# Two layers of graph attention and weighted sums on one core: GpSimd takes over the range guard's products, the sums' factors and the low features' split

## The chip, the cores and the metric

The kernel runs on one core of a Trainium2 chip. The metric is the device time of one execution in microseconds; the median of three runs is given. A separate profiled execution leaves the trace that is read below. The engines are named as in the profile: PE (matrix multiply), DVE (VectorE), ACT (ScalarE), POOL (GpSimd), SP (which issues the large loads).

## The reference

`x` is 3327 x 64, `adj` a symmetric 0/1 matrix of 3327 x 3327 with about 0.5% ones. Layer 0 aggregates in hyperbolic space with attention, layer 1 sums a node's last hundred neighbours with weights that halve from one neighbour to the next. Both have a layer norm and a ReLU ahead and a residual.

```python
# layer 0, h = relu(layernorm(x))
x_t = logmap0(h, c)                                   # c = 1 / r^2
left, right = x_t @ w_att[:D, 0], x_t @ w_att[D:, 0]
adj_att = sigmoid(left[:, None] + right[None, :] + b_att[0]) * adj
x_local = logmap(h[:, None, :], h[None, :, :], c)
support_t = einsum('ij,ijd->id', adj_att, x_local)
x = x + proj(expmap(h, support_t, c), c)
# layer 1, h = relu(layernorm(x))
support = h @ weight
rank = cumsum(adj != 0, axis=1); deg = rank[:, -1:]
k = minimum(deg, 100.0); pos = rank - (deg - k)
w = mask * where(pos > 0, 0.5 ** (k - pos), 0.0)
x = x + w @ support + bias
```

## The kernel before

The 3328 padded nodes are 26 blocks of 128. The output nodes i are cut into four strips of 8, 8, 6 and 4 blocks; inside a strip the source nodes j run from block 25 down to block 0. A round is one block j of a strip (two in the last strip), and there are 26 + 26 + 26 + 13 = 91 rounds. For a round the work is:

- SP loads the adjacency tile `ad` (`load`, five buffers).
- DVE turns it into a mask (`edges`, L622), PE counts later neighbours with it (`count`, L633 and L634), and DVE or ACT, mostly in turn, keeps the count (`read`, L656, L658, L660).
- ACT makes the attention as a tanh (`sigmoids`, L671); DVE multiplies it by the adjacency (`pair_one`, L676).
- PE forms a pairwise quantity from features of i and j (`products`, L688 and L689); ACT applies two Gelu functions to it (`gelu`, L881); DVE multiplies it in (`pair_two`, L681).
- PE sums it against the table `hw` of j (`total`, L701). `hw` holds, for each node, 64 scaled features and one more factor.

Only the stretch ahead of the rounds and their beginning are touched by the change. There, per-node statistics are made by small DVE operations on 128 x 26 elements (L790 to L802): `x2`, the squared norm, `bal`, `babs`, `nrm`. Then the features `zf` (L805) are made for groups of blocks: `first_i` (0 to 7), `last_j` (24, 25), `high` (16 to 23) and `low` (8 to 15). Each group is stored in half precision twice: `nu`, a copy, and `nz`, a half precision copy (`nz[.., 0]`) with what it leaves over (`nz[.., 1]`, a difference). For `low` these are L911 on DVE, L926 on ACT and L933 on DVE. PE transposes them into PSUM (`turned_to`, L813), and DVE and ACT copy the transposes to `ju` (L817) and `jz` (L818), which `products` reads. For block group `first_i` six DMAs on POOL's queue (L867) move `iz` and `iu` into `jz` and `ju`.

The factors of the table are `wn` (L913, L916) and `opx` (L914); L915 writes the table's last column, and seven products on POOL (L919) its 64 features, in the order in which the rounds need them.

The range guard decides whether the fast path may stand: it takes the largest `nrm`, the largest `c x2 nrm`, and the largest and smallest `bal` over all real nodes (`node` is 1 for them and 0 for the padding). `range_steps` makes these in the tile `st` in four portions of DVE work (L980 to L990), which `advance` hands out to rounds 2 and after; `in_range` brings the four columns to one flag in the last rounds.

The order of PE, DVE and ACT is the order of the program text, written out by hand (`manual_schedule` with `IN_ORDER`). POOL's and SP's instructions are ordered by a scheduler, so a line of POOL's work can stand earlier or later than its place in the text. `post` (L1021) makes the per-node end of each strip with many small POOL instructions beside the next strip's rounds.

Of the kernel before, what the change touches and what calls it, by code (L numbers as in the profile page):

```python
# [12 lines left out]
F32 = mybir.dt.float32  # L13
# [6 lines left out]
ALU = mybir.AluOpType  # L20
AX = mybir.AxisListType
PSUM = bass.MemoryType.PSUM

P = 128
N = 3327
NB = 26
NP = NB * P
D = 64
# [11 lines left out]
BIG, LATER, ACT, POOL = 4, 99, 100, 101  # L40
# [35 lines left out]
WA = 4.016768702491527  # L76
# [372 lines left out]
def fast(ctx, tc, x, adj_t, r, w_att, b_att, weight, bias, out, flag):  # L449

    nc = tc.nc
    V, A, G, T = nc.vector, nc.scalar, nc.gpsimd, nc.tensor
# [47 lines left out]
    node = const.tile([P, NB], F32, name="node")  # L500
# [4 lines left out]
    def scalar_col(name):  # L505
        return const.tile([P, 1], F32, name=name)

    inv_r, c_c, sqc, absr, maxnorm, c2_c, m2c, p2c, negc, zs_c, za_c, f_c = (
        scalar_col(n) for n in ("inv_r", "c_c", "sqc", "absr", "maxnorm", "c2_c", "m2c", "p2c", "negc", "zs_c", "za_c",
                                "f_c"))  # L510
# [15 lines left out]
    def wide(t, n):  # L526
# [3 lines left out]
    x2, bal, balm, nrm, left, right, sv, su, sk, ih = (  # L530
        const.tile([P, NB], F32, name=n)
        for n in ("x2", "bal", "balm", "nrm", "left", "right", "sv", "su", "sk", "ih"))
    hw = const.tile([P, NB, D + 1], F32, name="hw")
# [9 lines left out]
    post_pool = ctx.enter_context(tc.tile_pool(name="post", bufs=1))  # L543
    st = const.tile([P, 4], F32, name="st")
# [119 lines left out]
    def sigmoids(n, of=slice(None)):  # L664

        S = strips[rounds[n][0]]
        if n not in sg_of:
            sg_of[n] = work.tile([P, FMAX], F32, name="sg", bufs=SGB)
        sg = sg_of[n]
        for j in js(n)[of]:  # L670
            A.activation(part(n, sg, j), S.left[:, : S.F], AF.Tanh, bias=right[:, j : j + 1], scale=0.5)  # L671

    def pair_one(n):
        w = span(n)
        sg = sg_of[n][:, :w]
        V.scalar_tensor_tensor(sg, sg, 1.0, ad_of.pop(n)[:, :w], op0=ALU.add, op1=ALU.mult)  # L676

    def pair_two(n):
        w = span(n)
        sg = sg_of[n][:, :w]  # L680
        V.scalar_tensor_tensor(sg, pq_of.pop(n)[:, :w], WD, sg, op0=ALU.add, op1=ALU.mult)  # L681
# [39 lines left out]
    def small(name):  # L721
        return pre.tile([P, NB], F32, name=name)
# [10 lines left out]
    v, y = v2[:, 0], y2[:, 0]  # L733
# [41 lines left out]
    zf = pre.tile([P, NB, D], F32, name="sq")  # L775
    nz = pre.tile([P, NB, 2, D], F16, name="d")
# [97 lines left out]
    high, low = slice(16, 24), slice(8, 16)  # L874
# [35 lines left out]
    features(low)  # L910
    V.tensor_copy(nu[:, low, :D], zf[:, low])  # L911
    wn, opx = small("wn"), small("opx")
    V.tensor_scalar(wn, nrm, WA / 2, None, op0=ALU.mult)  # L913
    V.tensor_scalar(opx, x2, c_c, 1.0, op0=ALU.mult, op1=ALU.add)  # L914
    V.tensor_mul(hw[:, :, D], opx, wn)  # L915
    V.tensor_mul(wn, wn, y)  # L916
    for b in (24, 20, 16, 12, 8, 4, 0):
        n = min(4, NB - b)
        G.tensor_mul(hw[:, b : b + n, :D], rl[:, b : b + n], wide(wn[:, b : b + n], n))  # L919
# [3 lines left out]
    sigmoids(0)  # L923
    kept(p3, high, 0)
    pair_one(0)
    A.copy(nz[:, low, 0], zf[:, low])  # L926
    pair_two(0)
    for j in js(1):
        count(1, j)
    products(1)  # L930
    A.copy(left_b[:, : strips[0].F], pl[:, : strips[0].F])
    strips[0].left = left_b
    V.tensor_sub(nz[:, low, 1], zf[:, low], nz[:, low, 0])  # L933
    sigmoids(1)
    gelus(1)
    logits((high,))
# [39 lines left out]


    def range_steps():
        t1 = post_pool.tile([P, NB], F32, name="st1")
        V.tensor_mul(t1, nrm, node)  # L980
        V.tensor_reduce(st[:, 0:1], t1, AX.X, ALU.max)
        yield 2
        V.scalar_tensor_tensor(t1, x2, c_c, t1, op0=ALU.mult, op1=ALU.mult)
        V.tensor_reduce(st[:, 1:2], t1, AX.X, ALU.max)
        yield 2
        V.tensor_mul(t1, bal, node)
        V.tensor_reduce(st[:, 2:3], t1, AX.X, ALU.max)
        yield 2
        V.tensor_reduce(st[:, 3:4], t1, AX.X, ALU.min)
        V.tensor_scalar(st[:, 3:4], st[:, 3:4], -1.0, None, op0=ALU.mult)  # L990

    def in_range():
        pf = ps.tile([P, P], F32, name="pc")
# [270 lines left out]
    def add(j, wt, n):  # L1264
# [5 lines left out]
                 start=j == order[0], stop=j == NB - 1)  # L1270

    stages, rest_of_ahead = [Stage(range_steps())], last_of_ahead()
    range_end = in_range()
    load(LOADS)
# [175 lines left out]
@with_exitstack  # L1450
def gnn_kernel(
    ctx: ExitStack,
    tc: tile.TileContext,
    x: bass.AP,
    adj_t: bass.AP,
    r: bass.AP,
    w_att: bass.AP,
    b_att: bass.AP,
    weight: bass.AP,
    bias: bass.AP,  # L1460
    out: bass.AP,
):
    keep = ctx.enter_context(tc.tile_pool(name="keep", bufs=1))
    flag = keep.tile([1, 1], I32, name="flag")
    args = (x, adj_t, r, w_att, b_att, weight, bias, out)
    with ExitStack() as inner:
        fast(inner, tc, *args, flag)
    cond = tc.nc.values_load(flag)
    with tc.If(cond > 0):
        with ExitStack() as inner:  # L1470
            general(inner, tc, *args)
# [28 lines left out]
```

## Time and profile before

| what | us |
|---|---|
| three runs, median | 398.67 |
| lowest and highest of them | 398.03 and 398.76 |
| the profiled execution, its own time | 398.52 |
| its span, first to last instruction | 396.7 |
| busy PE, DVE, ACT | 350.1, 364.2, 348.5 |
| busy POOL | 143.2 |

The span is 1.8 us shorter than the time of that execution. The page gives each engine's busy time as a mean over stages that differ: a set-up to about 36 us, the rounds of four strips to about 345 us, and the second layer's sums to the end. DVE with 92% of the span, PE and ACT with 88% each are close to each other; POOL has 36%. A row of the timeline shows the start, the duration, the engine and the line, the operation, output and inputs with their shapes. The durations of neighbours on one engine overlap a little, so the distance between two starts is the better measure of what an instruction takes from its engine.

### The profile page before, as it was taken

The page shows a single profiled execution, that of the slowest core. Times are in us where ns is not written, and L with a number is a line of the kernel's source. Part 1 is how long each engine was busy: PE and PEld are TensorE (multiplying, and loading weights), DVE is VectorE, ACT ScalarE, POOL GpSimd, SP SyncE. Part 2 cuts the span into 40 slices and gives each one's busy share as a digit, 9 for nine tenths or more (in the row PEclk, how much of TensorE's full clock was granted, in tenths as well). Part 3 has the DMA queues.
Part 4 walks back from the last instruction along what each step waited for, and adds up shares of the span by engine and source line. Part 5 has one row for each costly group of instructions (what it writes and reads, how often), then busy time and mean ns, then how long its engine had stood idle before and what let it go on. Part 6 is the DMA issues. An engine that isn't in the chain of part 4 may idle for free.

```text
span 396.7 us, 4776 instructions
## 1 busy us (share of the span) xinstructions
PE 350.1 (88%) x1460; PEld 149.3 (38%) x1460; DVE 364.2 (92%) x551; ACT 348.5 (88%) x401; POOL 143.2 (36%) x279
## 2 busy tenths in 40 slices
PE   0067999999999899999998999999977899999892
PEld 0053333333333333333333354444433333344362
DVE  3999999999999999999999999999998999798941
ACT  2589999999999999999999999999988899697510
POOL 8136200000000166932133674851248678234100
PEclk9999999999999999999999999999999999999996
DMA  7314555455557455545445445555644430000022
GB/s 208 150 43 132 177 141 145 142 161 156 159 159 211 133 154 158 159 127 164 137 129 151 121 134 161 153 136 151 192 133 135 122 107 0 2 0 1 2 47 48
DMA packets 23299, 49.00 MB, mean 124 GB/s; under 512 B 8789, under 2 KB 9245, under 8 KB 23265
## 3 DMA queue, kind: packets, MB, share of 16 engines
q1 hardware_dynamic: 20993, 47.66, 41.2%
q10 hardware_dynamic: 1808, 0.46, 0.6%
q0 software_dynamic: 464, 0.49, 0.5%
q8 instruction: 13, 0.21, 0.2%
q14 instruction: 21, 0.17, 0.1%
HBM read 46.40 MB, written 0.87 MB: 119 GB/s over the span
## 4 chain that ended last, share of the span: by engine, by line
DVE 42%; ACT 25%; issue 15%; PE 13%; POOL 2%; DMA 1%; POOLq 0%; DVEq 0%; ACTq 0%
DVE sg L676 12%; DVE sg L681 12%; ACT pq L881 10%; ACT sg L671 7%; PE po L701 4%; DVE mask L622 3%; ACT behind_lo L656 2%; ACT behind_hi L656 2%; PE pc L633 1%; DMA x_sb<-in_x 1%; DVE behind_hi L660 1%; DVE behind_lo L660 1%; PE pc L634 1%; PE pq L688 1%; PE pq L689 1%
## 5 line engine op out<-in xcount | busy, mean ns | idle before, releaser
L881 ACT ACTIVATE pq<-pq 128x1024 f32<-128x1024 f32 (+1 forms) x182 | 173.7, 960 | 2.6 <-PE pq L689 0.8
L701 PE MATMUL po<-sg,hw 128*65 128x512 f32 (+1 forms) x364 | 159.7, 562 | 0.1
L681 DVE SCALAR_TENSOR_TENSOR sg<-pq,sg 128x1024 f32<-128x1024 f32 (+1 forms) x91 | 103.7, 1140 | 3.1 <-ACT pq L881 2.4
L676 DVE SCALAR_TENSOR_TENSOR sg<-sg,ad 128x1024 f32<-128x1024 f32 (+1 forms) x91 | 105.5, 1160 | 0.1
L671 ACT ACTIVATE sg<-left_b,right 128x1024 f32<-128x1024 f32 (+2 forms) x103 | 101.7, 987 | 0.0
L701 PEld LDWEIGHTS po<-sg,hw 128*65 128x65 f32 x364 | 48.9, 137 | 67.1 <-issue 52.8
L633 PE MATMUL pc<-mask,ca 128*128 128x512 bf16 (+1 forms) x175 | 63.5, 363 | 8.9 <-ACT behind_hi L656 3.5
L688 PE MATMUL pq<-iu,ju 71*128 71x512 f16 (+1 forms) x182 | 66.5, 366 | 1.1 <-ACT jz L818 0.8
L634 PE MATMUL pc<-mask,cb 128*128 128x512 bf16 (+1 forms) x182 | 64.7, 366 | 1.6 <-DVE mask L622 1.6
L689 PE MATMUL pq<-iz,jz 128*128 128x512 f16 (+1 forms) x182 | 65.0, 364 | 0.0
L622 DVE TENSOR_SCALAR mask<-ad 128x1024 bf16<-128x1024 f32 (+1 forms) x91 | 59.2, 652 | 0.0
L634 PEld LDWEIGHTS <-cb 128*128 128x128 bf16 x182 | 17.7, 97 | 47.5 <-issue 34.6
L1108 POOL CAST w<-mask 128x1 f32<-128x1 bf16 x3 | 1.5, 505 | 89.3 <-DVE mask L622 89.2
L633 PEld LDWEIGHTS <-ca 128*128 128x128 bf16 x175 | 17.1, 98 | 30.5 <-issue 18.3
L688 PEld LDWEIGHTS <-ju 71*128 71x128 f16 x182 | 17.8, 98 | 23.1 <-DVE sg L681 5.4
L1269 PEld LDWEIGHTS <-s 128*128 128x128 f16 x182 | 17.7, 98 | 21.3 <-DVE s L1093 2.3
L689 PEld LDWEIGHTS <-jz 128*128 128x128 f16 x182 | 17.9, 98 | 18.7 <-issue 1.1
L660 DVE TENSOR_SCALAR behind_lo<-pc 128x1024 uint8<-128x1024 f32 (+2 forms) x24 | 24.4, 1019 | 0.3 <-PE pc L634 0.3
L656 ACT ACTIVATE behind_hi<-pc 128x1024 uint8<-128x1024 f32 (+2 forms) x25 | 21.8, 873 | 1.6 <-PE pc L634 1.6
L656 ACT ACTIVATE behind_lo<-pc 128x1024 uint8<-128x1024 f32 (+2 forms) x24 | 20.8, 865 | 0.0
L852 PE MATMUL pq<-id,nui 128*71 128x128 f16 x8 | 1.0, 312 | 21.4 <-ACT nzi L826 21.4
L660 DVE TENSOR_SCALAR behind_hi<-pc 128x1024 uint8<-128x1024 f32 (+2 forms) x15 | 14.8, 985 | 0.9 <-PE pc L634 0.7
(344 smaller groups left out, 382.6 us busy)
## 6 DMA issues: line engine op xcount, KB each, us to landing
ad<-in_adj_t SPq DMA_DIRECT2D x65, 512.0 KB, 3.6
ad<-in_adj_t SPq DMA_DIRECT2D x26, 384.0 KB, 3.2
out<-o SPq DMA_DIRECT2D x6, 128.0 KB, 1.9
left_b<-left_d SPq DMA_DIRECT2D x1, 512.0 KB, 4.5
x_sb<-in_x ACTq DMA_DIRECT2D x1, 416.0 KB
x_sb<-in_x SPq DMA_DIRECT2D x1, 416.0 KB, 5.2
left_b<-left_d SPq DMA_DIRECT2D x1, 384.0 KB
jz<-iz POOLq DMA_DIRECT2D x2, 128.0 KB, 2.6
```

The costliest lines, as they stand in the source:

```text
L622: V.tensor_scalar(*args, 0.0, None, op0=ALU.not_equal)
L633: T.matmul(S.pc[:, f0:f1], ca, S.before[:, f0:f1], start=False, stop=True, skip_group_check=True)
L634: T.matmul(S.pc[:, f0:f1], cb, now[:, f0:f1], start=S.first, stop=True, skip_group_check=True)
L656: A.activation(kept, of, AF.Relu, scale=128.0 if j in JD else 1.0)
L660: V.tensor_scalar(kept, S.pc[:, : S.F], 0.0, None, op0=ALU.max)
L671: A.activation(part(n, sg, j), S.left[:, : S.F], AF.Tanh, bias=right[:, j : j + 1], scale=0.5)
L676: V.scalar_tensor_tensor(sg, sg, 1.0, ad_of.pop(n)[:, :w], op0=ALU.add, op1=ALU.mult)
L681: V.scalar_tensor_tensor(sg, pq_of.pop(n)[:, :w], WD, sg, op0=ALU.add, op1=ALU.mult)
L688: T.matmul(part(n, pq, j, f0, f1), ju[:KB, j, :], S.iu[:, f0:f1], start=True, stop=False)
L689: T.matmul(part(n, pq, j, f0, f1), jz[:, j, :], S.iz[:, f0:f1], start=False, stop=True)
L701: T.matmul(po[: D + 1, : f1 - f0], hw[:, j, :], part(n, sg_of[n], j, f0, f1), start=j == NB - 1, stop=j == 0)
L881: A.activation(pq, pq, AF.Gelu, scale=scale)
```

## The change

Three pieces of work move to POOL.

- The four instructions of the sums' factors (L913 to L916) are issued on POOL in place of DVE. The products of the table, already on POOL, come from them.
- The low features' half precision copy moves from ACT (L926) to POOL, and the difference from DVE (L933) to POOL, directly behind it.
- The range guard's products are made on POOL, side by side in one tile `tops` of 128 x 4 x 26. One DVE reduction makes all four columns of `st`; the smallest `bal` becomes the largest of the negated products. The portions of DVE work become one.

```diff
-    V.tensor_scalar(wn, nrm, WA / 2, None, op0=ALU.mult)
-    V.tensor_scalar(opx, x2, c_c, 1.0, op0=ALU.mult, op1=ALU.add)
-    V.tensor_mul(hw[:, :, D], opx, wn)
-    V.tensor_mul(wn, wn, y)
+    G.tensor_scalar(wn, nrm, WA / 2, None, op0=ALU.mult)
+    G.tensor_scalar(opx, x2, c_c, 1.0, op0=ALU.mult, op1=ALU.add)
+    G.tensor_mul(hw[:, :, D], opx, wn)
+    G.tensor_mul(wn, wn, y)
     for b in (24, 20, 16, 12, 8, 4, 0):
         n = min(4, NB - b)
         G.tensor_mul(hw[:, b : b + n, :D], rl[:, b : b + n], wide(wn[:, b : b + n], n))
...
     pair_one(0)
-    A.copy(nz[:, low, 0], zf[:, low])
+    G.tensor_copy(nz[:, low, 0], zf[:, low])
+    G.tensor_sub(nz[:, low, 1], zf[:, low], nz[:, low, 0])
     pair_two(0)
...
     strips[0].left = left_b
-    V.tensor_sub(nz[:, low, 1], zf[:, low], nz[:, low, 0])
     sigmoids(1)
...
     def range_steps():
-        t1 = post_pool.tile([P, NB], F32, name="st1")
-        V.tensor_mul(t1, nrm, node)
-        V.tensor_reduce(st[:, 0:1], t1, AX.X, ALU.max)
-        yield 2
-        V.scalar_tensor_tensor(t1, x2, c_c, t1, op0=ALU.mult, op1=ALU.mult)
-        V.tensor_reduce(st[:, 1:2], t1, AX.X, ALU.max)
-        yield 2
-        V.tensor_mul(t1, bal, node)
-        V.tensor_reduce(st[:, 2:3], t1, AX.X, ALU.max)
-        yield 2
-        V.tensor_reduce(st[:, 3:4], t1, AX.X, ALU.min)
-        V.tensor_scalar(st[:, 3:4], st[:, 3:4], -1.0, None, op0=ALU.mult)
+        tops = post_pool.tile([P, 4, NB], F32, name="tops")
+        G.tensor_mul(tops[:, 0], nrm, node)
+        G.tensor_scalar(tops[:, 1], x2, c_c, None, op0=ALU.mult)
+        G.tensor_mul(tops[:, 1], tops[:, 1], tops[:, 0])
+        G.tensor_mul(tops[:, 2], bal, node)
+        G.tensor_scalar(tops[:, 3], tops[:, 2], -1.0, None, op0=ALU.mult)
+        yield LATER
+        V.tensor_reduce(st, tops, AX.X, ALU.max)
+        yield LATER
```

In the changed build the orders of PE, DVE and ACT are those of before without the moved instructions, and with the one reduction at the place of the guard's second portion. On POOL the scheduler puts the factors, the guard's products and then the seven products of the table directly behind the first small instructions, and ahead of the six DMAs of L867; the low features' copy and difference stand behind these DMAs. On SP one adjacency load stands ahead of the third strip's own loads instead of between them.

## The prediction

> **What bounds the kernel now.** I read the busy time by stretches first, to see which engine is full where the change acts and which is full afterwards.
>
> ```profile
> 18.00:24.00 6.00, 2.50 (x21) 2.30 (x22) 5.62 (x29) 4.39 (x11) 0.51 (x2) 1.00 0.01 1
> 24.00:29.30 5.30, 4.37 (x51) 2.73 (x50) 5.06 (x20) 4.45 (x7) 3.20 (x6) 1.00 0.31 79
> 29.30:36.20 6.90, 4.99 (x43) 2.42 (x42) 6.83 (x12) 6.42 (x7) 6.69 (x7) 1.00 0.27 78
> 43.80:127.00 83.20, 82.27 (x284) 31.04 (x283) 82.39 (x92) 82.40 (x85) 1.80 (x2) 1.00 0.54 160
> 127.00:208.00 81.00, 79.91 (x283) 30.57 (x282) 80.80 (x84) 80.27 (x86) 33.29 (x64) 1.00 0.51 148
> ```
>
> The columns are the stretch, its length, then PE, PEld, DVE, ACT and POOL. In the set-up, 18 to 36 us, DVE is full (5.62 of 6.00, 5.06 of 5.30, 6.83 of 6.90). POOL works 0.51 us before 24 us and is full from 29.3 to 36.2. After 43.8 us three engines are full at once. Which one sets the pace is in ACT's timeline, followed by the only line that the waits of ACT hold between 44 and 210 us:
>
> ```profile
> 46.72 1.14 ACT L671 ACTIVATE sg<-left_b,right 128x1024 f32<-128x1024 f32 x1
> 47.76 2.06 ACT L881 ACTIVATE pq<-pq 128x1024 f32<-128x1024 f32 x2
> 49.73 1.14 ACT L671 ACTIVATE sg<-left_b,right 128x1024 f32<-128x1024 f32 x1
> 50.77 1.01 ACT L656 ACTIVATE behind_hi<-pc 128x1024 uint8<-128x1024 f32 x1
> 51.67 2.06 ACT L881 ACTIVATE pq<-pq 128x1024 f32<-128x1024 f32 x2
> 53.65 1.14 ACT L671 ACTIVATE sg<-left_b,right 128x1024 f32<-128x1024 f32 x1
> ...
> ACT behind_hi L656 <- PE pc L634: 0.3, 1, 0.3
> ```
>
> Two rounds take ACT 53.65 - 46.72 = 6.93 us, exactly its own work, and in 166 us it waits 0.3 us. So from 43.83 us (that one wait) to about 208 us ACT is the bound. What the set-up gains or loses moves ACT's start and is carried on whole; what DVE saves in the rounds only makes DVE wait. The chain of waits draws the range guard's steps (L980 to L990, 51 to 63 us) through DVE, but the even period shows that ACT doesn't feel them.
>
> The set-up's path, from the same chain: DVE's small operations to 19.2, ACT, PE's transposes, DVE's copy of iu at 23.80 (queued behind L622, which ended at 23.68, so with 0.1 us of slack), DVE without a gap to 36.23, and then the copy of the low features' transposes:
>
> ```profile
> 33.09 0.90 DVE d L933
> 34.50 1.13 DVE sg L676
> 36.26 1.02 ACT jz L818
> ```
>
> Everything up to 43.83 hangs on that copy at 36.26.
>
> Last, what DVE and POOL do to each other:
>
> ```profile
> 26.88 0.68 DVE L904 TENSOR_TENSOR d<-sq,d 128x512 f16<-128x512 f32 x1
> 33.01 0.99 DVE L933 TENSOR_TENSOR d<-sq,d 128x512 f16<-128x512 f32 x1
> 353.06 1.22 DVE L1380 TENSOR_SCALAR wt<-behind_lo 128x1664 uint16<-128x1664 uint16 x1
> 364.69 0.87 DVE L1078 TENSOR_TENSOR rt_last<-rn_last 128x4 f32<-128x4 f32 x1 [0.42 <-POOL rn_last L1078]
> ```
>
> L904 and L933 are one operation on one shape: 0.68 us with POOL issuing DMAs, 0.99 us beside the table's products. L1380 takes 0.58 us elsewhere and 1.22 beside a POOL product of 384; a product of four elements, 0.16 us elsewhere, took 0.87 beside POOL's subtraction of 364.64. The loss is no slower rate, but a wait for the POOL instruction to end.
>
> **What the Trainium skill says.** SBUF — State Buffer, section "Who interferes with whom": DVE's second read port is GpSimd's only one; a DVE instruction with two SBUF inputs, or in a two-port mode, and a GpSimd instruction that reads SBUF exclude each other: "the other fully blocks". The four rows agree (+0.31, +0.64, +0.71 us). It also says that a PSUM operand keeps DVE out of this: L681 at 31.87 took its usual 1.23 us beside the products. Perfetto Trace Analysis, "GPSIMD Engine Instruction", advises the spacing of starts rather than durations for GpSimd; I do so. GPSIMD Engine Reference, "Engine selection", has GpSimd about two times slower for two inputs; the products here are far off that path, so the ratio isn't used.
>
> **The change, part by part.** The instruction order of the changed build shows more than the diff: on POOL the eleven small operations (four of the factors, five of the guard, two older copies) and all seven table products now stand ahead of the six DMAs of L867. Before, the products came behind them.
>
> (a) Removed from DVE: L913 to L916, 28.54 to 29.24 = 0.70 us; L933, 0.90 us in place. Removed from ACT: the copy at L926, 0.52 us start to start (31.46 to 31.98). Beside the products at their old place DVE also loses 0.19 us (L676 at 30.44: 1.40 against 1.21) which goes; L933's 0.31 is in its 0.90.
>
> (b) The guard: eight DVE instructions of 0.15 to 0.24 us at four places against one reduction of 128x4x26 (estimate 0.25 us; L981 takes 0.18 for 26 elements). About 1.2 us of DVE, worth 0, since ACT sets the pace there. Bounds: 0, and a gain of 1.2 if DVE did set it.
>
> (c) The small operations on POOL. Inputs arrive at 17.94 (x2), 18.22, 18.45 and 18.80 us (nrm). POOL's small instructions start 0.16 us apart when independent (320.10 to 320.26) and 0.29 apart when one needs the other (146.50, 146.80, 147.09). Five and six of them: 2.5 us, with DVE between them some 3.3, so the products begin at about 21.3 us and not 29.41. DVE's chain of 18.0 to 19.2 meets some six of them; bounded by 0 (POOL's four of 15.7 to 16.3 left no trace on DVE) and 6 x 0.12 = 0.7; I take 0.3.
>
> (d) The products, the term that decides. Their starts in narrow windows are 0.57 us apart when free (30.15, 30.72), and L933, started at 33.01 against a product of 32.84, ran as if begun at 33.31: a product holds the port 0.47 us. Seven of them (the first is half as long) now fall between 21.3 and some 27 us. There DVE has L840, L843, L844, L845, L846 (two SBUF inputs), L841, L842 (half precision copies, uncertain) and L622 (the mask[...]) in a row, and L860 behind them. Whoever waits is served when the other ends, as at 353.06 (DVE, POOL, DVE), so each DVE instruction pays up to one product. Most: 7 x 0.47 = 3.2 us. Least: the products run while DVE reads PSUM or waits for PE (1.4 us from 23.8 on) and it is 0.5, as at the old place. I take six meetings at 0.38, between the 0.30 of L933 and the full 0.47: 2.3 us. With (c), L860 comes 2.6 us later, and everything behind it: PE's products, the gelu of round 0, sigmoids.
>
> (e) What (a) gives back of it on the path. At L676 of round 0 (30.44) DVE would be 2.6 - 0.7 = 1.9 later, but ACT's sigmoid, which lost nothing, 2.6: ACT is late next. ACT then drops L926 (0.52) and its 0.34 us wait for L817: its copy to left_b, the sigmoid and gelu of round 1 and the copy at 36.26, which starts 0.14 us after that gelu, are 2.6 - 0.52 - 0.34 - 0.14 = 1.6 us later. DVE: L676 of round 1 follows the sigmoid, L817 ends about 37.6, within the 37.86 of that copy.
>
> (f) The low features on POOL: products done about 26.5, the six DMA issues took 3.2 us (24.78 to 27.99) and start when iu is there, 27.2, so to 30.5; the low features are ready at 28.17 + 2.6 = 30.8; copy 0.5 (estimate from L489's 0.34 for 128 columns), subtraction 1.0 to 1.8 (364.64: 0.91 for 384; 1.54 and 1.82 for 512 with waits). Done at 32.4 to 33.3, 4 us ahead of the copy of their transposes: cost 0. Its cover gone, each us late would be a us. L926's and L933's readers are PE's transposes alone. The six DMAs, 2.5 us later, fill ju and jz for blocks 0 to 7, which the first strip reads last (about 100 us): 0. On SP one adjacency load moves ahead of the third strip's loads near 120 us; the data are needed some 10 us later: 0.
>
> **Sum.** +0.3 + 2.3 - 1.0 = +1.6 us. Profiled execution: 398.52 us (span 396.7 and 1.8 around it) to 400.1; the median of the runs shown is 398.67, 0.15 above: 400.3. The bounds: (c) 0 to 0.7 and (d) 0.5 to 3.2, less 1.0, give -0.5 to +2.9.
>
> **Rivals.** "Same" is within 0.2%, 0.8 us, about what this kernel's measurement can tell.
> 1. Forecast: the products hold DVE up at 21 to 27 us; +0.9 to +2.9, 399.6 to 401.6. For it: the four rows and the order. Against: no row shows a run of small DVE instructions between products. Chance 0.64.
> 2. The products slip into DVE's waits and PSUM reads. It decides once fewer than three meetings of 0.4 are left: 0.3 + 0.9 - 1.0, about +0.2: 398.9, from -0.7 to +0.7. Chance 0.16.
> 3. The other side, faster: DVE keeps the port from 18 to 29 us and POOL waits, so only (a) counts. The point is a loss in (c) and (d) under 0.2 us; then -0.86 to -1.0, and up to -2.2 if the guard's 1.2 counts also: 397.7, from 396.5. For it: DVE is never idle there. Against: a POOL instruction that has begun isn't interrupted (364.69). Chance 0.14.
> 4. POOL is so late that the transposes wait for its subtraction: 402 to 404, chance 0.06.
>
> Faster 0.14, same 0.17 (case 2 and the edge of 1), slower 0.69. The range leaves out case 3 and most of 4: 398.0 to 401.9; the forecast's own is 399.6 to 401.6.
>
> **What would show it.** The first product on POOL near 21 us; L843 to L846 or L622 with 0.3 to 0.5 us above their times; L860 at 25.5 to 27 against 23.80; the copy of L818 for the low features near 37.9 against 36.26; ACT's period still 6.93 and its start in the rounds shifted alike; DVE with idle time behind 66 us. If L860 stands at 24 and that copy before 36, case 3 holds. If ACT's period shortens, (b) was wrong.

## The result, and the profile after

The changed kernel takes 400.76 us (median of ten runs, 400.35 to 402.29) against 399.12 us (ten runs, 397.44 to 400.80) for the kernel before beside it: 1.0056 times as long, 95% interval 1.0036 to 1.0076, so about 1.4 to 3.0 us slower. (The ratio is taken over all these runs; it is not the quotient of the two medians, which is 1.0041, or 1.64 us.) The profiled execution took 400.45 us with a span of 398.6, against 398.52 and 396.7 before.

The busy time by stretches of the changed kernel, in the columns of the forecast (start and end, length, PE, PEld, DVE, ACT, POOL, granted clock, DMA share, GB/s):

```profile
18.00:24.00 6.00, 2.50 (x20) 2.10 (x21) 5.92 (x23) 4.27 (x11) 5.74 (x16) 1.00 0.00 1
24.00:29.30 5.30, 3.30 (x28) 1.63 (x28) 5.05 (x16) 2.53 (x5) 3.70 (x8) 1.00 0.20 44
43.80:127.00 83.20, 82.07 (x282) 31.50 (x286) 82.36 (x87) 82.09 (x84) 2.34 (x4) 1.00 0.54 163
```

DVE is full at 18 to 24 us as before, but works on 23 instructions there in place of 29. In 24 to 29.3 us PE does 28 matmuls in place of 51, and ACT 2.53 us of work in place of 4.45: both wait. From 43.8 us on the columns are close to those of before.

What fills DVE is in its own timeline. The kernel before, then the changed one:

```profile
21.46 0.69 DVE L840 TENSOR_TENSOR nzi<-sq,nzi 128x512 f16<-128x512 f32 x1 [0.16 <-ACT nzi L826]
22.07 0.23 DVE L841 COPY nu<-nu 128x78 f16<-128x78 f16 x1
22.17 0.23 DVE L842 COPY nu<-nu 128x78 f16<-128x78 f16 x1
22.28 0.28 DVE L843 TENSOR_TENSOR d<-sq,d 128x128 f16<-128x128 f32 x1
22.47 0.18 DVE L844 SCALAR_TENSOR_TENSOR g<-g,s 128x26 f32<-128x26 f32 x1
22.56 0.24 DVE L845 SCALAR_TENSOR_TENSOR g<-g,g 128x26 f32<-128x26 f32 x1
22.92 0.25 DVE L846 SCALAR_TENSOR_TENSOR g<-g,g,g 128x26 f32<-128x26 f32 x1
23.08 0.69 DVE L622 TENSOR_SCALAR mask<-ad 128x1024 bf16<-128x1024 f32 x1
23.80 0.69 DVE L860 COPY iu<-pq 71x1024 f16<-71x1024 f16 x1
```

```profile
21.19 0.78 DVE L840 TENSOR_TENSOR nzi<-sq,nzi 128x512 f16<-128x512 f32 x1
21.90 0.63 DVE L841 COPY nu<-nu 128x78 f16<-128x78 f16 x1
22.41 0.22 DVE L842 COPY nu<-nu 128x78 f16<-128x78 f16 x1
22.52 0.69 DVE L843 TENSOR_TENSOR d<-sq,d 128x128 f16<-128x128 f32 x1
23.14 0.59 DVE L844 SCALAR_TENSOR_TENSOR g<-g,s 128x26 f32<-128x26 f32 x1
23.65 0.65 DVE L845 SCALAR_TENSOR_TENSOR g<-g,g 128x26 f32<-128x26 f32 x1
24.41 0.46 DVE L846 SCALAR_TENSOR_TENSOR g<-g,g,g 128x26 f32<-128x26 f32 x1
24.80 1.16 DVE L622 TENSOR_SCALAR mask<-ad 128x1024 bf16<-128x1024 f32 x1
25.88 0.68 DVE L860 COPY iu<-pq 71x1024 f16<-71x1024 f16 x1
```

From L840 to L622 the extra durations are 0.09, 0.40, none, 0.41, 0.41, 0.41, 0.21 and 0.47: 2.40 us. An operation of 26 columns pays as much as one of 128: the wait has the size of what POOL is doing, not of what DVE does. POOL's timeline says what that is:

```profile
21.02 4.38 POOL L919 TENSOR_TENSOR hw<-rl,wn 128x128 f32<-128x128 f32 x7
26.85 0.62 POOL L867 DMA_DIRECT2D ju<-iu  x1 [1.44 <-DVE yr L872]
...
30.32 0.86 POOL L926 CAST d<-sq 128x512 f16<-128x512 f32 x1
31.26 1.48 POOL L927 TENSOR_TENSOR d<-sq,d 128x512 f16<-128x512 f32 x1
```

The seven table products lie over exactly these DVE instructions, and L860, the copy that all later work waits for, follows them. How much of it reaches the rounds is in ACT's timeline:

```profile
37.42 1.01 ACT L818 COPY jz<-pq 128x1024 f16<-128x1024 f16 x1
...
45.00 1.02 ACT L656 ACTIVATE behind_hi<-pc 128x1024 uint8<-128x1024 f32 x1 [0.34 <-PE pc L634]
...
47.89 1.14 ACT L671 ACTIVATE sg<-left_b,right 128x1024 f32<-128x1024 f32 x1
...
54.82 1.14 ACT L671 ACTIVATE sg<-left_b,right 128x1024 f32<-128x1024 f32 x1
```

L818 was at 36.26 and L656 at 43.83: ACT enters the rounds 1.17 us late, keeps its period of 54.82 - 47.89 = 6.93 us, and the shift stays: 125.89 became 127.08, 208.27 became 209.49, and PE's last closing matmul went from 388.50 to 389.66 (+1.16). Two things lie outside of the shift. The operations around L801 came earlier in this profile (L801 on DVE at 18.68 instead of 18.99), ahead of nearly all that the change touches. And the span ends 8.94 us after the last closing matmul, not 8.20 as before. So the span is 1.47 us longer from L801 to the last matmul, 0.31 shorter ahead of L801 and 0.74 longer behind the last matmul: 1.9 us in all.

### The profile page after: what moved, and what is told of

Its sections match the earlier page's. It is cut to its first block, busy times and chain, and to the rows that moved or that the text cites. A ratio compares the mean times of both kernels' runs of the same rounds, so it can differ in the third digit from the quotient of the medians.

```text
span 398.6 us, 4753 instructions
## 1 busy us (share of the span) xinstructions
PE 349.9 (88%) x1436; PEld 150.7 (38%) x1460; DVE 365.3 (92%) x539; ACT 348.1 (87%) x400; POOL 146.1 (37%) x290
## 4 chain that ended last, share of the span: by engine, by line
DVE 34%; ACT 34%; issue 16%; PE 11%; POOL 2%; DMA 1%; POOLq 0%; DVEq 0%; ACTq 0%
ACT pq L881 13%; ACT sg L671 10%; DVE sg L676 9%; DVE sg L681 9%; PE po L701 4%; ACT behind_hi L656 3%; DVE mask L622 3%; ACT behind_lo L656 2%; PE pc L633 1%; DMA x_sb<-in_x 1%; DVE behind_lo L660 1%; PE pc L634 1%; PE pw L1426 1%; ACT weight_of L656 1%; PE pw L1266 1%
## 5 line engine op out<-in xcount | busy, mean ns | idle before, releaser
L681 DVE SCALAR_TENSOR_TENSOR sg<-pq,sg 128x1024 f32<-128x1024 f32 (+1 forms) x91 | 103.6, 1138 | 3.7 <-ACT pq L881 2.8
L676 DVE SCALAR_TENSOR_TENSOR sg<-sg,ad 128x1024 f32<-128x1024 f32 (+1 forms) x91 | 105.4, 1158 | 0.2
L671 ACT ACTIVATE sg<-left_b,right 128x1024 f32<-128x1024 f32 (+2 forms) x103 | 101.7, 988 | 0.0
L633 PE MATMUL pc<-mask,ca 128*128 128x512 bf16 (+1 forms) x170 | 61.6, 362 | 9.5 <-ACT behind_hi L656 4.3
L689 PE MATMUL pq<-iz,jz 128*128 128x512 f16 (+1 forms) x182 | 65.5, 367 | 0.0
L634 PE MATMUL pc<-mask,cb 128*128 128x512 bf16 (+1 forms) x168 | 59.6, 365 | 3.1 <-DVE mask L622 2.1
L622 DVE TENSOR_SCALAR mask<-ad 128x1024 bf16<-128x1024 f32 (+1 forms) x91 | 59.9, 659 | 0.0
L689 PEld LDWEIGHTS <-jz 128*128 128x128 f16 x182 | 18.0, 99 | 19.6 <-issue 1.5
L656 ACT ACTIVATE behind_hi<-pc 128x1024 uint8<-128x1024 f32 (+2 forms) x25 | 21.8, 873 | 1.5 <-remote 0.8
L656 ACT ACTIVATE behind_lo<-pc 128x1024 uint8<-128x1024 f32 (+2 forms) x24 | 20.8, 867 | 0.0
```

Source lines behind the costliest of these rows:

```text
L622: V.tensor_scalar(*args, 0.0, None, op0=ALU.not_equal)
L633: T.matmul(S.pc[:, f0:f1], ca, S.before[:, f0:f1], start=False, stop=True, skip_group_check=True)
L634: T.matmul(S.pc[:, f0:f1], cb, now[:, f0:f1], start=S.first, stop=True, skip_group_check=True)
L656: A.activation(kept, of, AF.Relu, scale=128.0 if j in JD else 1.0)
L689: T.matmul(part(n, pq, j, f0, f1), jz[:, j, :], S.iz[:, f0:f1], start=False, stop=True)
```

## The experiments

L801 started anywhere from 18.25 to 19.05 us in the profiles below, with and without the change's parts, so places are given from L801 on. The table has the three that the theories speak of: L860 on DVE, the low features' L818 on ACT, and the last closing matmul on PE; the last column is the ratio of the times to the kernel before on the same chip, with its 95% interval.

| kernel | L860 | L818 | last matmul | time, before beside it | ratio |
|---|---|---|---|---|---|
| before | 4.81 | 17.27 | 369.51 | | |
| changed | 7.20 | 18.74 | 370.98 | 400.76, 399.12 | 1.0056 (1.0036 to 1.0076) |
| e1_factors | 7.02 | 19.44 | 372.86 | 401.20, 398.58 | 1.0065 (1.004 to 1.009) |
| e2_guard | 4.93 | 17.56 | 371.41 | 398.73, 398.58 | 1.0007 (0.9993 to 1.002) |
| e3_low_first | 4.81 | 18.82 | 371.66 | 399.97, 398.58 | 1.003 (1.0018 to 1.0042) |
| e4_held | 5.00 | 16.81 | 368.57 | 398.52, 398.58 | 0.9996 (0.9982 to 1.001) |
| e5_one | 7.42 | 19.87 | 372.10 | 401.69, 398.66 | 1.0073 (1.0057 to 1.009) |
| e9_three | 5.67 | 17.65 | 369.91 | 400.02, 398.66 | 1.0044 (1.0027 to 1.0061) |
| e7_held_only | 4.80 | 17.57 | 371.46 | 398.70, 398.81 | 1.000 (0.9986 to 1.0015) |
| e6_guard_more | 4.81 | 17.26 | 370.59 | 400.12, 398.66 | 1.0051 (1.0032 to 1.0071) |
| e11_guard_some | 4.80 | 17.25 | 369.57 | 399.53, 398.81 | 1.0022 (1.0007 to 1.0037) |
| e8_act_order | 5.00 | 16.72 | 370.63 | 399.12, 398.66 | 1.001 (0.9997 to 1.0023) |
| e10_no_gate | 5.00 | 16.74 | 370.14 | 398.41, 398.81 | 0.9996 (0.9979 to 1.0014) |
| e12_no_guard | 4.85 | 17.50 | 369.74 | 397.76, 398.59 | 0.9978 (0.9964 to 0.9992) |

The last matmul of e1, e2, e7, e8 and e10 holds some 1.7 us of another kind, told at the end. From L818 to the last matmul it takes 352.23 to 352.26 us in before, the changed kernel, e5, e9 and e12, with and without the guard's change. So the delay at L818 is carried on whole, and what else the change moved behind it, the later six DMAs and the load on SP, cost nothing.

**The factors alone (e1).** The kernel before with one edit:

```diff
-    V.tensor_scalar(wn, nrm, WA / 2, None, op0=ALU.mult)
-    V.tensor_scalar(opx, x2, c_c, 1.0, op0=ALU.mult, op1=ALU.add)
-    V.tensor_mul(hw[:, :, D], opx, wn)
-    V.tensor_mul(wn, wn, y)
+    G.tensor_scalar(wn, nrm, WA / 2, None, op0=ALU.mult)
+    G.tensor_scalar(opx, x2, c_c, 1.0, op0=ALU.mult, op1=ALU.add)
+    G.tensor_mul(hw[:, :, D], opx, wn)
+    G.tensor_mul(wn, wn, y)
```

> The kernel before with one part of the change: only the factors of the sums are made on GpSimd, so that the seven table products move to about 21 to 25.5 us, in front of the six transfers. Theory P (the products hold the port that VectorE shares, and that alone decides): VectorE's operations L840 to L846 and the mask of round 1 are stretched by about 0.4 us each, L860 starts at 25.9 to 26.3 us instead of 23.80, the copy of the low features L818 at 37.3 to 38.3 instead of 36.26, and the time is 1.0 to 2.0 us above before. Rival R1 (the low features' work on GpSimd decides) and rival R3 (the guard decides): no later L860, time within 0.4 us of before. Rival R2 (the small operations on GpSimd decide): L860 later by under 0.7 us.

The products ran from 19.89 to 24.35 us, L840 took 1.10 and L843 0.70, and L860 came 2.21 us later after L801 than before. (At 25.42 us it missed the written 25.9 to 26.3, because this set-up began early.) The products came 0.85 us sooner after L801 than in the changed kernel and met L835 to L844 instead; the mask L622, expected to be stretched too, kept its 0.69 us. L818 at 37.84 is as expected; the time, 1.6 to 3.6 us above, reaches beyond the 2.0. One part of three gives the whole loss, and the seven products in it are no new work: they only start earlier.

**The guard alone (e2).** `range_steps` as changed, all else as before.

> The kernel before with another part alone: only the range guard changed, its products on GpSimd in the set-up and one reduction on VectorE later. Theory P with ScalarE setting the pace: the five small operations on GpSimd cost under 0.3 us at L860 (23.8 to 24.1), L818 starts at 36.2 to 36.6, and the 0.9 us taken from VectorE in the rounds bring nothing: time within 0.5 us of before, and the first regular count on ScalarE (L656) no more than 0.4 us from 43.83. Rival R2 (small operations on GpSimd cost): L860 at 24.3 or later, time up by 0.6 or more. A bound by VectorE in the rounds: 0.6 to 1.2 us faster, the gain arising between 44 and 120 us.

L860 is 0.12 us later, the time the same, and ACT's period 6.93 us (L671 at 55.67 and 62.60): neither a price of the small operations on POOL nor a gain from DVE's shorter guard. L656 missed its place, 45.86 instead of within 0.4 of 43.83, for a reason outside of the theories (last section).

**The low features alone (e3).** Their copy and difference on POOL, the products held behind the mask of round 1:

```diff
+    edges(1)
+    G.tensor_copy(nz[:, low, 0], zf[:, low])
+    G.tensor_sub(nz[:, low, 1], zf[:, low], nz[:, low, 0])
+    wny = small("wny")
+    G.tensor_copy(wny[:, :1], mask_of[1][:, :1])
+    G.tensor_copy(wny, wn)
...
-        G.tensor_mul(hw[:, b : b + n, :D], rl[:, b : b + n], wide(wn[:, b : b + n], n))
-    edges(1)
+        G.tensor_mul(hw[:, b : b + n, :D], rl[:, b : b + n], wide(wny[:, b : b + n], n))
...
-    A.copy(nz[:, low, 0], zf[:, low])
...
-    V.tensor_sub(nz[:, low, 1], zf[:, low], nz[:, low, 0])
```

> The kernel before with the third part alone: the low features' half precision copy and their difference on GpSimd, issued ahead of the table products, which are held until the mask of round 1 is there, so that they begin at about 32 us instead of 29.4. Theory P: L860 stays at 23.8; ScalarE loses 0.52 and VectorE 0.7 to 0.9 us of work before the copy L818, against up to 0.6 us more by which the products stretch VectorE's L676 and L681: L818 at 35.4 to 36.3, time 0 to 0.9 us under before. Rival R1 (the low features come too late from GpSimd for the transposes): the copy L818 at 37 us or later and time 0.8 us or more above before.

I was wrong: 0.7 to 1.7 us slower, with L818 at 37.29. The number is that of rival R1, the mechanism is not (part of L818's delay is a slow stretch of PE from 32.4 us on in this profile, as in the last section). DVE's timeline:

```profile
28.02 0.58 DVE L913 TENSOR_SCALAR wn<-nrm 128x26 f32<-128x26 f32 x1
28.52 0.23 DVE L914 TENSOR_SCALAR opx<-x,c_c 128x26 f32<-128x26 f32 x1
28.78 1.09 DVE L915 TENSOR_TENSOR hw<-opx,wn 128x26 f32<-128x26 f32 x1
29.90 0.19 DVE L916 TENSOR_TENSOR wn<-wn,y 128x26 f32<-128x26 f32 x1
30.01 0.69 DVE L622 TENSOR_SCALAR mask<-ad 128x1024 bf16<-128x1024 f32 x1
```

L913 and L915 took 0.17 and 0.20 us before. POOL's cast ran at 27.71 and its difference from 28.66 to 29.81, until L915 was let through. The low features were ready; the mask of round 1 was 1.29 us late after L801 (11.54 against 10.25), and PE waited 2.25 us for it. It is the port again, with other work on both sides: the four instructions that the change takes away from DVE are the ones that POOL's low split holds up here. So the parts don't add up one by one; this part alone costs more than it does in the company of the first.

**The products held (e4).** The changed kernel with the low split first and the products behind the mask of round 1:

```diff
-    G.tensor_mul(wn, wn, y)
+    G.tensor_copy(nz[:, low, 0], zf[:, low])
+    G.tensor_sub(nz[:, low, 1], zf[:, low], nz[:, low, 0])
+    edges(1)
+    wny = small("wny")
+    G.tensor_copy(wny[:, :1], mask_of[1][:, :1])
+    G.tensor_mul(wny, wn, y)
     for b in (24, 20, 16, 12, 8, 4, 0):
         n = min(4, NB - b)
-        G.tensor_mul(hw[:, b : b + n, :D], rl[:, b : b + n], wide(wn[:, b : b + n], n))
-    edges(1)
+        G.tensor_mul(hw[:, b : b + n, :D], rl[:, b : b + n], wide(wny[:, b : b + n], n))
...
     pair_one(0)
-    G.tensor_copy(nz[:, low, 0], zf[:, low])
-    G.tensor_sub(nz[:, low, 1], zf[:, low], nz[:, low, 0])
```

> The changed kernel with all its parts, only that the table products are held behind the mask of round 1, after the low features' copy and difference; the small operations on GpSimd stay where the change put them. Theory P: L860 returns to 23.5 to 24.1 us, L818 starts at 35.2 to 36.2, and the time is 0.2 to 1.0 us under before (1.4 to 2.6 under the changed kernel). Rival R2 (the small operations decide): L860 stays at 25 or later. Rival R1 (the low features on GpSimd are late): L860 early but L818 at 37 or later, time still 1 us above before.

All small operations stand where the change put them, and L860 is back within 0.19 us, L840 to L846 at their old durations. L818 comes 1.93 us earlier than in the changed kernel. That separates the products from the small operations (R2) and from the low features (R1). The time, though, was expected under before and is the same, between 0.7 us below and 0.4 above, while the last matmul of the profile comes 0.94 us earlier. Of that 0.46 is at L818; the other 0.48 arises only between 293 and 305 us, in this profile alone of the undisturbed ones, and is not shown to come from the edit. The span ends 8.78 us after the last matmul, 0.58 later than before.

**One product, three products, and the old place (e5, e9, e7).** e5 has one product over all 26 blocks in place of the loop. e9 leaves the products of blocks 24, 20 and 16 in front and holds the other four as e4 does. e7 is the kernel before with only the holding of e3.

> The changed kernel with one table product of all 26 blocks in place of the seven; everything else as changed. If GpSimd gives the shared port back only when an instruction ends (theory P, as the forecast read it), VectorE meets one long hold in place of seven: L840 or L841 waits for 2.5 to 4 us in one piece and the operations after it run at their own length, with L860 7.0 to 8.5 us after L801 (before 4.81, changed 7.20) and the time 1.5 to 3 us above before. If the two engines merely share the rate, L840 to L846 are each stretched by a like factor. If the sevenfold meeting was the whole cost and the hold itself is short, L860 comes back to under 6 us after L801 and the time within 0.8 us of before.

> The changed kernel with the first three of the seven products where the change puts them (10 of the 26 blocks, about 1.7 us of GpSimd) and the other four held behind the mask of round 1. Theory P, a price per product: three meetings in place of six or seven, L860 at 5.6 to 6.3 us after L801 (before 4.81, changed 7.20, all seven held 5.00), the low features' L818 at 17.2 to 18.0 (held 16.81, changed 18.74), time 0.3 to 1.3 us above before. If it were not the products but what else the change puts ahead of 21 us, L860 stays at 7 or later; if the first products slip into gaps, at 5.2 or earlier.

> The kernel before with nothing moved but its seven table products, held behind the mask of round 1 (after two small copies on GpSimd), where before they began at 29.4 us. Theory P, in which ScalarE's run from 25 us on is the bound and VectorE has some slack beside it: L860 4.7 to 5.0 us after L801, the low features' copy L818 at 17.0 to 17.8 (before 17.27), time within 0.5 us of before. If a product costs VectorE and the end 0.4 us wherever it lies, the delay is there in both places and nothing changes either; but if the later place were the worse one, L818 at 18 or later and time 0.7 us or more above.

The one product settles how the two engines share. First DVE, then POOL:

```profile
21.55 3.35 DVE L840 TENSOR_TENSOR nzi<-sq,nzi 128x512 f16<-128x512 f32 x1
24.82 0.22 DVE L841 COPY nu<-nu 128x78 f16<-128x78 f16 x1
...
25.04 0.27 DVE L843 TENSOR_TENSOR d<-sq,d 128x128 f16<-128x128 f32 x1
```

```profile
21.38 2.98 POOL L917 TENSOR_TENSOR hw<-rl,wn 128x1664 f32<-128x1664 f32 x1
```

L840 starts 0.17 us after the product, stands until the product ends at 24.36, and is done 0.54 us later; the next ones have their own length. So here the two do not share by rate: one waits for the end of the other. Seven pieces or one, the loss is nearly the same (L860 at 7.20 and 7.42), since DVE pays for the length of the holds either way; e5's time, 2.3 to 3.6 us above, is at and beyond the upper end of what was expected. With three products in front (10 of 26 blocks) L860 comes at 5.67: 0.09, 0.40 and 0.42 us at L840, L841 and L843, and none on what follows up to L860; its time, 1.1 to 2.4 us above, is at and beyond the upper end of what was expected. And the later place costs no more than the old one: e7 takes the time of before.

**How much of DVE's time the rounds feel (e6, e11).** In the kernel before, each of the guard's four reductions is repeated on DVE twice (e6) or once (e11) more into a tile that nobody reads, in e6 with the sign change of the last one as well, like this:

```diff
         V.tensor_reduce(st[:, 0:1], t1, AX.X, ALU.max)
+        V.tensor_reduce(again[:, 0:1], t1, AX.X, ALU.max)
+        V.tensor_reduce(again[:, 0:1], t1, AX.X, ALU.max)
```

> The kernel before with each of the range guard's four reductions done three times instead of once on VectorE, the additional results unused: nine operations more, 1.3 to 1.7 us of VectorE's time between 50 and 70 us. Theory P with ScalarE setting the pace in the rounds: time within 0.6 us of before, though VectorE is 96 per cent busy or more there. If VectorE sets the pace: 1.2 to 1.7 us slower.

> The kernel before with each of the guard's four reductions done twice instead of once: 0.5 to 0.7 us more on VectorE in the rounds instead of the 1.25 us of the run before, which came out 0.63 us late on ScalarE by 88 us. If ScalarE sets the pace and VectorE runs up to about 0.6 us behind it at no cost: ScalarE within 0.15 us of its places before, time within 0.4 us of before. If VectorE sets the pace at every size: ScalarE 0.5 to 0.7 us late by 90 us, time 0.5 to 0.8 above.

e6 was expected at no cost and is 1.3 to 2.8 us slower. DVE's L676 of 66.17 us moved to 67.42, 1.25 later. ACT in e6, then in the kernel before:

```profile
70.58 1.14 ACT L671 ACTIVATE sg<-left_b,right 128x1024 f32<-128x1024 f32 x1
...
74.60 1.14 ACT L671 ACTIVATE sg<-left_b,right 128x1024 f32<-128x1024 f32 x1
...
78.05 1.14 ACT L671 ACTIVATE sg<-left_b,right 128x1024 f32<-128x1024 f32 x1
```

```profile
70.50 1.14 ACT L671 ACTIVATE sg<-left_b,right 128x1024 f32<-128x1024 f32 x1
...
74.42 1.14 ACT L671 ACTIVATE sg<-left_b,right 128x1024 f32<-128x1024 f32 x1
...
77.43 1.14 ACT L671 ACTIVATE sg<-left_b,right 128x1024 f32<-128x1024 f32 x1
```

ACT is on time until 67 us, then 0.08, 0.18 and 0.62 us late: it waited 0.35 us for PE's products (L689), and PE for DVE's L681. That holds through the first strip. In the second ACT waits for L689 again, 0.40 us at 140 us, and the last matmul is 1.08 us later: of the 1.25 us nearly all was felt in the end. In e11 the addition was smaller than planned, 0.24 us at the L676 of 66.17 us (counted from L801). In its profile ACT is on time at 126 us (107.92 after L801, 107.94 before) and the last matmul within 0.06 us, but the timed runs are 0.3 to 1.5 us slower. These two don't agree, and that some of DVE's time is free to add is not shown. That adding 1.25 us costs is; and taking 1.1 us away brings nothing (e2: 1.26 us from start to start for the old guard, 0.17 for the new one).

**Further on (e8, e10, e12).** e8 is e4 with two things earlier on ACT: round 0's count ahead of the high features' copy (and of its difference on DVE), and `left_b` ahead of `kept(p3, high, 0)`. e10 is e8 with the products held by the low difference (`G.tensor_copy(wny[:, :1], nz[:, low.start, 1, :1])`). e12 is e4 with `range_steps` as before.

> The version with the held products, and on ScalarE two things in another order: the first count of round 0 ahead of the high features' copy, which waits for VectorE, and the copy of the turned left factors ahead of the copy L818 of the high features. If ScalarE's unbroken run from 25 us on sets the end, its first Gelu starts 7.3 to 7.7 us after L801 instead of 8.33, the low features' L818 at 15.9 to 16.6 instead of 16.81, and the time is 0.3 to 1.4 us under before. If VectorE (the masks and L676 stretched by GpSimd) or the transposes are as late, the Gelu is early but L818 stays at 16.7 or later and the time stays within 0.4 us of before.

> The version with the held products and ScalarE's other order, with the products held behind the low features' difference on GpSimd itself in place of VectorE's mask, so that GpSimd's small copy of the mask, which took 1.71 us there, no longer stands ahead of that difference. If that copy made the low features late: the difference is done by 31.7 us after the start in place of 32.8, the low features' L818 starts 15.7 to 16.4 us after L801 instead of 16.72, and the time is 0.2 to 1.2 us under before. If the stretched masks and L676 on VectorE are the limit: L818 stays at 16.6 or later and the time within 0.4 us of before.

> The version with all seven products held, only that the range guard is as in the kernel before, on VectorE. In the profiles so far the time from the last closing matmul to the end of the span was 8.56 to 9.08 us in all seven kernels with the guard changed and 8.11 to 8.47 in five of the six without. If the guard's change has a price there, this kernel ends 8.1 to 8.5 us after its last matmul and its time is 0.4 to 1.2 us under before, with L818 16.6 to 17.0 us after L801. If that end only varies from program to program, it may be 8.6 or more here, and the time within 0.4 us of before. If VectorE's 0.9 us of guard in the rounds costs in this version, the last closing matmul is 0.3 us or more later against L801 than with the guard changed (368.57).

In e8 the first Gelu is early (7.48), as wanted, and L818 isn't: it waits 0.99 us for DVE's L817. In e10 POOL's difference is done by 30.4 us and L818 waits 1.00 us all the same. DVE, through L676 and L817, is as late as ACT was: L818 gains 0.1 us, and neither run shows a gain in time.

e12 is faster than the kernel before, by 0.3 to 1.4 us: 397.76 against 398.59. It ends 8.34 us after its last matmul, as was expected of a kernel with the old guard. L818 missed its place (17.50), as PE was slow at 25 to 30 us in this profile and L817 waited 0.90 us for the transposes. The profile doesn't show where the gain lies: after L801 its last matmul is 0.23 us later than before. It is also 1.17 us later than in e4, where an added 0.3 or more was to mean that the guard costs on DVE; but 0.69 of that is at L818, and the other 0.48 is what e4 alone had gained near 300 us. Whether the guard's change costs anything is still open: the intervals of e4 and e12 overlap, e2 against before shows nothing, and e6, with the old guard, had 8.93 us at the end as well. After PE's last matmul the traces hold two additions on DVE and the output's transfer, whose packets end 4.2 to 5.4 us after that matmul; then come single fetches of instructions (queue q14) and time in which no engine is busy. Why the end is longer in some kernels they don't show. This version keeps two parts of the change, the factors and the low split, and puts the table products back behind the set-up.

## Why the prediction was right

It said 400.3 us with a slowdown by the products on the shared port, and the time was 400.76. Of its signs all came but one, the idle time of DVE (b). By its steps:

(a) The removed instructions are gone, with one exception in what was credited: the 0.19 us of L676 did not come back (1.42 us in the changed kernel, 1.40 before), for POOL's difference for the low features now stands beside it where a product stood.

(b) The guard worth 0: shown by e2. The reason given for it, that ACT is the bound and DVE only waits, was too strong. DVE was to have idle time behind 66 us. The same columns for 66 to 127 us, before and changed, say that it has none (61.00 of 61.00 us):

```profile
66.00:127.00 61.00, 60.93 (x212) 23.22 (x211) 61.00 (x64) 60.42 (x63) 0.00 (x0) 1.00 0.55 163
66.00:127.00 61.00, 60.79 (x209) 23.42 (x212) 61.00 (x63) 60.43 (x62) 0.00 (x0) 1.00 0.54 162
```

Two rounds take DVE 6.87 us from L676 to L676 (70.17 to 77.04 before) and ACT 6.93, so DVE hardly makes up for a delay. e6 shows it: 1.25 us more are felt. The zero was right for a removal only.

(c) The small operations on POOL: 0.3 foreseen, nothing found. L840 comes 2.51 us after L801 in the changed kernel, 2.51 in e4 and 2.47 in e2 and before.

(d) Six meetings at 0.38, or 2.3 us: five meetings at 0.40 to 0.47, one of 0.21 at L846 and 0.09 at L840, 2.40 in sum. e1 gives the loss with nothing else changed, e4 takes it away with all else in place, e9 gives the fraction, and e5 shows that it is a wait and no shared rate. The order in which both engines alternate was taken from one pair of instructions near 353 us; it held. The Trainium skill, SBUF — State Buffer, "Who interferes with whom", says that the two exclude each other where a VectorE instruction has two SBUF inputs or is in a two-port mode, and not where it has at most one SBUF input outside of these modes, as with a second input from PSUM; here the exclusion is seen in both directions and for the half precision copy L841 (0.23 to 0.63 us) as well, which the forecast had left uncertain.

(e) 1.0 given back on the way to L818: 2.39 at L860 became 1.47 at L818, so 0.92. ACT had been late next, as foreseen: between its sigmoid L671 (2.46 us late after L801) and L818 it gained 0.27 us on the wait for L817, 0.52 by the dropped copy and 0.20 behind the gelu, where 0.34, 0.52 and 0.14 were expected.

(f) The low features in time: POOL's difference ended at 32.74 us, foreseen at 32.4 to 33.3. But "cost 0" counted only the lateness. The two instructions also hold the port: the mask of round 1 took 1.10 us instead of 0.68. In the changed kernel that was hidden, as ACT was late already; in e3, where it met L913 to L916, it cost 1.29 us.

Sum: +1.6 foreseen, +1.47 from L801 to the last matmul. The remaining 0.4 us of the profile's 1.9 (less 0.31 ahead, plus 0.74 after) are in no step. The forecast counted from 398.67, the median of the first three runs of before; the ten have 399.12, and the two medians differ by 1.64. The size of (d) was worked out and came; that the 0.3 of (c), which was not found, stands against 0.2 more in (d) and (e) together, and that the timed difference is nearer to 1.6 than the profile's 1.9, is luck. Rival 2 (few meetings), rival 3 (POOL waits) and rival 4 (late transposes) all fall with the lines above.

## What to carry to other kernels

Work that is handed to GpSimd is priced by what it delays on VectorE while it runs, not by whether VectorE's own list gets shorter. Follow what a move makes ready earlier: the factors were small, but the large products that hung on them came forward by 8 us, into the one stretch where VectorE had short operations in a row on the path; holding them back dropped the loss, and with the guard left on VectorE as well the kernel was 0.3 to 1.4 us faster than before (e12). And test a "this engine is the bound" in both directions: that taking work from the other engine gains nothing doesn't mean that giving it work is free (e2 and e6).

## What the runs showed of the hardware beyond that

The hold works against GpSimd too. Its copy of one column, and a product of 26 columns, in e8:

```profile
29.96 1.71 POOL L920 CAST wny<-mask 128x1 f32<-128x1 bf16 x1 [0.61 <-DVE mask L622]
...
32.76 0.23 POOL L921 TENSOR_TENSOR wny<-wn,y 128x26 f32<-128x26 f32 x1
```

The copy took 1.71 us and ended as VectorE's L676 did (30.42 to 31.63); in e4 it took 0.19, and there the product, 0.23 us here, took 1.21. By its record the copy began 0.46 us ahead of L676, and in both kernels 0.14 us after L817 did: who gets the port first can't be read from the starts, and why it differs these traces don't show. A hold by GpSimd is long: e5's product of 1664 columns took 2.98 us, 1.8 ns a column.

TensorE has slow stretches of its own. In five profiles (e1, e2, e7, e8, e10) its 512-column matmuls took 0.63 us instead of 0.38 for some 2 to 4 us between 38 and 45 us; of e2:

```profile
39.63 0.38 PE L633 MATMUL pc<-mask,ca 128*128 128x512 bf16 x1
39.88 0.47 PE L634 MATMUL pc<-mask,cb 128*128 128x512 bf16 x1
40.14 0.63 PE L633 MATMUL pc<-mask,ca 128*128 128x512 bf16 x1
...
42.28 0.63 PE L689 MATMUL pq<-iz,jz 128*128 128x512 f16 x1
42.70 2.26 PE L701 MATMUL po<-sg,hw 128*65 128x512 f32 x4
44.80 0.38 PE L633 MATMUL pc<-mask,ca 128*128 128x512 bf16 x1
```

The granted clock of 36 to 44 us was 0.79 there (0.79 to 0.81 in the five) and 1.00 in the profiles of before and after. ACT's count L656 then waits 2.0 us for PE instead of 0.35, and this 1.7 us is carried to the end. Four of these five kernels are not measurably slower than before in their timed runs. In e3 and e11 such a stretch lies between 31 and 37 us (granted clock 0.63 and 0.72 from 30 to 36 us). Several profiles, the changed kernel's among them, have a shorter one at 25 to 30 us (27.39 to 29.2 in the changed one, where PE had been left with little to do), where L817 waits up to 0.9 us for PE (e5, e12). The starts of the slow ones are 0.43 us apart, of the others 0.22 (38.75 and 38.97). The Trainium skill, TensorE: Matmul & The Clock Gate, Part 1, "The HAM clock gate", gives these two distances (426.7 and 215.7 ns) for TensorE at half and at full clock, and has the clock fall back after an idle window, one that runs freely, so that the place of a change differs from run to run. The distances agree; the window itself no trace here shows, and for the stretches at 25 to 30 us the column of the granted clock says 1.00 in spite of the same distances. I read the stretches as a part of the scatter of single executions, not of these kernels. The place of L860, ahead of all these stretches, is what tells the theories apart most safely.
